# Attention block on one core: group weights in two tiles, a pinned division, v's products in seven of eight key blocks

## The chip, the core and the metric

The kernel runs on one NeuronCore of a Trainium2 chip, in 32-bit floats throughout. The metric is the device time in microseconds of one execution; the profile is one execution under the hardware profiler. Five engines work side by side, each with its own instruction stream: TensorE (PE; its weight loads are shown as PEld), VectorE (DVE), ScalarE (ACT), GpSimd (POOL) and SyncE (SP), which here only issues DMAs. A 32-bit matmul shows as two instructions (two passes) in the trace, so that a product of 128x512 counts twice.

## The reference

Sixteen images `x` of 512 channels and 32 x 32 = 1024 positions go through one attention block. Cut to what is computed:

```python
xn  = (x - mean) * rsqrt(var + 1e-5)          # over each of 8 groups of 64 channels
xn  = xn * gamma + beta
q, k, v = split(qkv_w @ xn + qkv_b)           # each 512 x 1024
# 4 heads of 128 channels
attn = softmax(q.T @ k / sqrt(128))           # 1024 x 1024 for each head
o    = v @ attn.T
out  = x + proj_w @ o + proj_b
```

## The kernel before

**Loop.** The program is one unrolled sequence of steps: image `b` (16), head `h` (4), key block `j` (8 blocks of 128 keys). A step computes `scores` (line 710: 128 keys against 1024 queries in two halves, exponential on ScalarE, running sum of the exponentials `tot` on VectorE at lines 724 and 726) and the `weighted_sum` (line 801) of the step before. After a head's last block, `denominators` (line 728) turns the sum into a 32x32 tile of reciprocals; `spread_inverse` (line 751) writes it to a DRAM row and loads it back to all partitions (`rinv`, DMAs on ScalarE's queue); `divide` (line 815) multiplies the head's output `o` by it, on VectorE. The sums of the projection's operand (`sums_of_b`, line 268, shown as L272 on `o` and `ot`) read the divided outputs.

**Filler.** Between the attention's matmuls stand the projections of other images: q and k of the image's second pair of heads in head 0, the output projection of the image before in head 1, q and k of the next image's first pair in head 2, v of the next image in head 3. `plan_head` (line 947) spreads the units of such a projection over the eight blocks with `spread(plan, units, first, last)` (line 818): unit i goes to block first + i(last - first)/n.

**Projections.** Each is two levels of Strassen's scheme (Winograd's form, seven products in place of eight). The seven outer products go in four groups, `OUTER = ((1, 5), (2, 6), (7, 4), (3,))`: two, two, two and one at a time. A group is `two_levels`' unit list (line 457): seven inner products in the order 1, 2, 6, 5, 7, 4, 3, each followed by its eviction from PSUM (line 421 on ScalarE, line 529 on VectorE) and by outstanding additions (`combine`, line 572). Thus a projection has 28 units; a unit of the last group is half as large. `staggered` (line 842) starts group 1 when group 0 has done four units, group 2 four later, group 3 eight after that, so two groups overlap. Sums of the moving operand are made by VectorE at line 495 (`qk_t`, `pp_t`), or, for v, loaded back from DRAM where q and k of the same image kept them. v's results go through an addition (line 649, `vt`), a 32x32 transpose (line 652, `vu`), a DRAM tile (`vd`) and a load in another order (line 665).

**Weights.** A group's weights are one tile of seven 128x128 blocks for each of its outer products: the four raw blocks a11, a12, a21, a22 and the sums s1, s2, s3, s4, where s3 takes a21's place (`SLOTS`). In image 0 `group_weights` (line 345) makes them from staged raw blocks with VectorE (lines 355 to 375) and stores them in DRAM; later every group loads its tile with one DMA on SyncE's queue (line 350). The pool `w` has two buffers, shared by the groups of all projections:

```python
wpool = ctx.enter_context(tc.tile_pool(name="w", bufs=2))
FACTORS = {1: ("a11", "b11"), 2: ("a12", "b21"), 3: ("s4", "b22"), 4: ("a22", "t4"),
           5: ("s1", "t1"), 6: ("s2", "t2"), 7: ("s3", "t3")}
```

(The first line is line 171; the table is lines 142 to 145.) A tile's buffer comes free when the last product that reads the tile is done, and SyncE's load of a later group waits for that.

**Order.** The framework orders each engine's instructions when the program is built: a planner simulates the engines, takes what it believes to be ready first, and may put an instruction far ahead of its place in the source. On the chip each engine then runs its list in that fixed order and waits at the head of it. `tc.issue_after(ins)` makes the instructions of its block come after `ins` in their engine's list.

Of the kernel before, what the change touches and what calls it, by code (L numbers as in the profile page):

```python
# [10 lines left out]
F32 = mybir.dt.float32  # L11
# [5 lines left out]
P = 128  # L17
# [126 lines left out]
    5: ("s1", "t1"), 6: ("s2", "t2"), 7: ("s3", "t3"),  # L144
}

SLOTS = {"a11": 0, "a12": 1, "a21": 2, "s3": 2, "a22": 3, "s1": 4, "s2": 5, "s4": 6}
KC = 2
Q = 256

# [4 lines left out]
def fast_path(ctx, tc, x, sources, out, consts, flag, dims):  # L155
# [6 lines left out]
    nc = tc.nc  # L162
# [150 lines left out]
    stage, store = {}, {}  # L313
    for site in (*range(PAIRS), "proj", "v"):
        for g, group in enumerate(OUTER):
            store[site, g] = kept.tile(
                [P, len(group), 7, P], F32, name=f"kept_{site}_{g}"
            )

    store["last"] = kept.tile([P, 8, HALF], F32, name="kept_last")  # L320

# [22 lines left out]

    def group_weights(site, g, first):

        group = OUTER[g]
        w = wpool.tile([P, 2, 7, P], F32, tag="w", name=f"w_{site}_{g}")
        if not first:
            nc.sync.dma_start(w[:, : len(group)], store[site, g])  # L350
            return w
        st, raw = stage[site], raw_blocks(site)
        for i, p in enumerate(group):
            n = FACTORS[p][0]
            flat = w[:, i, 0:4, :].rearrange("p s d -> p (s d)")
            if n in raw:
                load_block(w[:, i, 0:4, :], raw[n])
            elif n == "s1":
                nc.vector.tensor_add(flat, st["a21"], st["a22"])
            elif n == "s2":  # L360
                nc.vector.tensor_sub(flat, st["s1"], st["a11"])
            elif n == "s3":
                nc.vector.tensor_sub(flat, st["a11"], st["a21"])
            else:
                nc.vector.tensor_sub(flat, st["a12"], st["s2"])
            if site == "proj":
                nc.sync.dma_start(store["last"][:, p], flat)

        def at(n):
            return w[:, : len(group), SLOTS[n], :]  # L370

        nc.vector.tensor_add(at("s1"), at("a21"), at("a22"))
        nc.vector.tensor_sub(at("s3"), at("a11"), at("a21"))
        nc.vector.tensor_sub(at("s2"), at("s1"), at("a11"))
        nc.vector.tensor_sub(at("s4"), at("a12"), at("s2"))
        nc.sync.dma_start(store[site, g], w[:, : len(group)])
        return w

    wv = {}
# [77 lines left out]
    def two_levels(name, site, b, blocks, finish, sums="make"):  # L457

        R = {}
        haves = [{} for _ in OUTER]

        def part(g, i, row=None):
            t = R[g][:, i]
            return t if row is None else t[:, row, :]

        def group_units(g):
            group = OUTER[g]
            n = len(group)  # L470
            have = haves[g]

            def weights():
                have["w"] = group_weights(site, g, b == 0 and site in range(PAIRS))

            def sum_tile(h, m):
                haves[h][m] = tpool.tile(
                    [P, 2, Q], F32, tag=f"in_{m}", name=f"{name}_{h}_{m}"
                )
                return haves[h][m][:, : len(OUTER[h])]  # L480

            def load(h, m):
                if sums == "load" and h < len(OUTER):
                    nc.sync.dma_start(sum_tile(h, m), inner_kept[b, h, m])

            def inner_sum(m):
                if sums == "load":
                    return
                sum_tile(g, m)
                a, c = {  # L490
                    "t1": ("b12", "b11"), "t2": ("b22", "t1"), "t3": ("t2", "b11"),
                    "t4": ("b21", "t2"),
                }[m]
                for i in range(n):
                    nc.vector.tensor_sub(have[m][:, i, :], inner(i, a), inner(i, c))  # L495
                if sums == "keep":
                    t = dpool.tile([P, n, Q], F32, tag=f"{m}_{g}", bufs=1, name=f"kept_{m}_{g}")
                    inner_kept[b, g, m] = t
                    nc.gpsimd.dma_start(t, have[m][:, :n])  # L499

            def inner(i, m):
                if m[0] == "t":
                    return have[m][:, i, :]
                outer = blocks()[FACTORS[group[i]][1]]
                return outer[int(m[1]) - 1][:, ts(int(m[2]) - 1, Q)]

            def mm(acc, j, first):
                an, bn = FACTORS[j]
                for i in range(n):
                    nc.tensor.matmul(  # L510
                        acc[:, ts(i, Q)], have["w"][:, i, SLOTS[an], :], inner(i, bn),
                        start=(first and i == 0), stop=True, skip_group_check=True,
                    )

            def out_(which, a, c=None):
                row, half = int(which[1]) - 1, int(which[2]) - 1
                if g not in R:
                    R[g] = rpool.tile(
                        [P, 2, 2, HALF], F32, tag=f"r{g % 3}", name=f"{name}_r{g}"
                    )  # L520
                dst = R[g][:, :n, row, ts(half, Q)]

                def view(t):
                    return t[:, : n * Q].rearrange("p (i q) -> p i q", q=Q)

                if c is None:
                    nc.scalar.copy(dst, view(a))
                else:
                    nc.vector.tensor_add(dst, view(a), view(c))  # L529

            p1, p2, p6, p5, p7, p4, p3 = strassen(f"{name}_{g}", mm, out_, n * Q)

            def unit(*steps):
                def one():
                    for f in steps:
                        f()
                    for _ in range(min(len(pending), 2 if g == len(OUTER) - 1 else 1)):
                        pending.pop(0)()
                return one

            def end():
                combine(g)
                if g == len(OUTER) - 1:
                    run(pending)
                    pending.clear()


            return [
                unit(weights, lambda: inner_sum("t1"), lambda: inner_sum("t2"), p1),
                unit(lambda: inner_sum("t3"), p2), unit(lambda: inner_sum("t4"), p6),  # L550
                unit(lambda: load(g + 1, "t2"), p5), unit(lambda: load(g + 1, "t1"), p7),
                unit(lambda: load(g + 1, "t3"), p4),
                unit(lambda: load(g + 1, "t4"), p3, end),
            ]

        def first_loads():
            for m in ("t2", "t1", "t3", "t4"):
                t = tpool.tile([P, 2, Q], F32, tag=f"in_{m}", name=f"{name}_0_{m}")
                haves[0][m] = t
                nc.sync.dma_start(t, inner_kept[b, 0, m])  # L560

        pending = []

        def add(o, i, j):
            pending.append(lambda: nc.vector.tensor_add(part(*o), part(*i), part(*j)))

        def done(which, i, j):
            pending.extend(
                lambda r=r: finish(which, r, part(*i, r), part(*j, r)) for r in range(2)
            )  # L570

        def combine(g):

            if g == 1:
                done("c11", (0, 0), (1, 0))
                add((1, 1), (0, 0), (1, 1))
                add((1, 0), (1, 1), (0, 1))
            elif g == 2:
                add((2, 0), (1, 1), (2, 0))
                done("c22", (2, 0), (0, 1))  # L580
                done("c21", (2, 0), (2, 1))
            elif g == 3:
                done("c12", (1, 0), (3, 0))

        ahead[name] = first_loads
        return [group_units(g) for g in range(len(OUTER))]
# [113 lines left out]


    ps, tot, po, rinv, last_eviction = {}, {}, {}, {}, {}
    inverse, rows_of = {}, {}
    steps = B * HEADS * NB

    def where(s):
# [3 lines left out]
    def scores(s, half):  # L710
# [11 lines left out]
        if j == 1:  # L722
            tot[b, h] = lpool.tile([P, N], F32, tag="tot", name=f"tot_{b}_{h}")
            nc.vector.tensor_add(tot[b, h], ps[s - 1], ps[s])
        else:
            nc.vector.tensor_add(tot[b, h][:, i], tot[b, h][:, i], ps[s][:, i])  # L726

    def denominators(b, h):

# [217 lines left out]
    def plan_head(b, h):  # L947
# [39 lines left out]
        elif h == 2:  # L987
            spread(plan, staggered(qk_groups(b + 1, 0)), 0, NB)
        else:
            spread(plan, staggered(next_v.pop()), 0, NB)  # L990
        return plan

    def warm(n, name):
# [31 lines left out]
    for s in range(steps + 1):  # L1025
# [14 lines left out]
        for half in range(NH2):  # L1040
            if s < steps:
                scores(s, half)
                if j == 1 and s > NB:
                    spread_inverse(*where(s - NB)[:2], half)
                if half == 0 and j == 5 and s > NB:
                    divide(*where(s - NB)[:2])
            if s > 0:
                weighted_sum(s - 1, half)
            n = (len(units) + 1) // 2
# [137 lines left out]
```

## Time and profile before

| what | value |
|---|---|
| median of 8 runs | 3311.57 us (3307.72 to 3318.35) |
| the profiled execution | 3314.3 us, of which the span from first to last instruction is 3312.5 |
| mean granted clock of TensorE | 0.995 |
| TensorE matmul | 3206.3 us busy |
| VectorE | 2659.6 us busy |
| ScalarE | 1446.5 us busy |
| load of a group's weights, 896 KB, for q and k (90 times) | 6.2 us from issue to landing (median) |
| same for v / for the output projection (45 times each) | 4.9 / 4.4 us |
| inverse of the denominators, 512 KB (63 times) | 4.5 us from issue to landing (median), 12.3 at most |
| division of a head's output, 128x1024 (63 times) | 1.22 us |
| v's transposes, 128x512 (120 times) | 1.12 us |

A busy TensorE is not one at its peak, since matmuls are pipelined and their ends are modelled: starts tell more. A wait row such as "A L1 <- B L2: total, times, longest" says how long engine A stood idle before an instruction of line 1 until B's work of line 2 was done. Idle time of an engine costs nothing unless another one waits for it.

### The profile page before, as it was taken

The page shows a single profiled execution, that of the slowest core. Times are in us where ns is not written, and L with a number is a line of the kernel's source. Part 1 is how long each engine was busy: PE and PEld are TensorE (multiplying, and loading weights), DVE is VectorE, ACT ScalarE, POOL GpSimd, SP SyncE. Part 2 cuts the span into 40 slices and gives each one's busy share as a digit, 9 for nine tenths or more (in the row PEclk, how much of TensorE's full clock was granted, in tenths as well). Part 3 has the DMA queues.
Part 4 walks back from the last instruction along what each step waited for, and adds up shares of the span by engine and source line. Part 5 has one row for each costly group of instructions (what it writes and reads, how often), then busy time and mean ns, then how long its engine had stood idle before and what let it go on. Part 6 is the DMA issues. An engine that isn't in the chain of part 4 may idle for free. (4 is left out here: it accounts for less than half of the span.)

```text
span 3312.5 us, 33607 instructions
## 1 busy us (share of the span) xinstructions
PE 3206.3 (97%) x10474; PEld 2169.9 (66%) x10474; DVE 2659.6 (80%) x4609; ACT 1446.5 (44%) x2709; POOL 527.0 (16%) x938
## 2 busy tenths in 40 slices
PE   8999999999999999999999999999999999999999
PEld 6566666666666666666666666666666666666664
DVE  8878878788787887878888787887878878788784
ACT  2534435354353443534435354353534535344342
POOL 1011121111211112111121111212112121121100
PEclk9999999999999999999999999999999999999999
DMA  5555454545535455454554545545355463454631
GB/s 196 199 186 153 168 177 143 167 150 170 170 137 170 145 176 162 158 165 140 173 175 154 169 130 184 162 157 176 133 175 175 145 204 123 162 165 162 185 124 39
DMA packets 172664, 530.54 MB, mean 160 GB/s; under 512 B 28864, under 2 KB 51904, under 8 KB 172480
## 3 DMA queue, kind: packets, MB, share of 16 engines
q1 hardware_dynamic: 91120, 276.86, 25.3%
q0 software_dynamic: 67392, 216.07, 20.1%
q10 hardware_dynamic: 13968, 35.41, 3.4%
q8 instruction: 85, 1.39, 0.2%
q14 instruction: 99, 0.81, 0.1%
HBM read 389.56 MB, written 138.67 MB: 159 GB/s over the span
## 5 line engine op out<-in xcount | busy, mean ns | idle before, releaser
L806 PE MATMUL po<-p,v 128*128 128x512 f32 x2048 | 1056.2, 597 | 0.0
L713 PE MATMUL s<-qk,qk 128*128 128x512 f32 x2048 | 1052.8, 596 | 2.6 <-ACT p L718 2.5
L718 ACT ACTIVATE p<-s 128x512 f32<-128x512 f32 x1024 | 610.1, 596 | 994.3 <-PE s L713 989.3
L806 PEld LDWEIGHTS po<-p,v 128*128 128x128 f32 x2048 | 601.1, 303 | 317.8 <-issue 199.7
L726 DVE TENSOR_TENSOR tot<-tot,p 128x1024 f32<-128x1024 f32 x385 | 469.9, 1221 | 118.9 <-ACT p L718 116.9
L713 PEld LDWEIGHTS s<-qk,qk 128*128 128x128 f32 x2048 | 388.9, 191 | 91.8 <-issue 29.2
L510 PE MATMUL qk_x<-qk_t,w 128*128 128x256 f32 x1344 | 361.7, 386 | 2.3 <-DVE qk_t L495 1.2
L510 PEld LDWEIGHTS qk_x<-qk_t,w 128*128 128x128 f32 x1344 | 247.0, 190 | 175.7 <-issue 66.4
L421 ACT COPY qk_u<-qk_x 128x512 f32<-128x512 f32 (+1 forms) x256 | 136.3, 533 | 288.1 <-PE qk_x L510 246.1
L499 POOL DMA_DIRECT2D kept_t<-qk_t x256 | 138.8, 543 | 495.5 <-DVE qk_t L495 461.5
L660 POOL DMA_DIRECT2D vd<-vu x120 | 66.5, 554 | 827.6 <-DVE vu L652 767.4
L529 DVE TENSOR_TENSOR qk_r<-qk_y,qk_u 128x512 f32<-128x512 f32 (+1 forms) x256 | 158.5, 619 | 45.6 <-ACT qk_u L421 24.6
L510 PE MATMUL pp_x<-pp_t,w_proj 128*128 128x256 f32 x630 | 173.8, 389 | 2.8 <-ACT pp_u L421 2.8
L529 DVE TENSOR_TENSOR v_r<-v_y,v_u 128x512 f32<-128x512 f32 (+1 forms) x120 | 74.9, 624 | 124.9 <-ACT v_u L421 117.3
L510 PE MATMUL qk_y<-qk_t,w 128*128 128x256 f32 x448 | 130.7, 398 | 43.4 <-DVE qk_t L495 29.7
L697 POOL DMA_DIRECT2D out_y<-y x120 | 66.4, 554 | 653.4 <-DVE y L696 620.6
L510 PEld LDWEIGHTS v_x<-v_t,w_v 128*128 128x128 f32 x630 | 118.4, 190 | 79.1 <-issue 38.3
L510 PE MATMUL v_x<-v_t,w_v 128*128 128x256 f32 x630 | 166.6, 381 | 0.0
L510 PEld LDWEIGHTS pp_x<-pp_t,w_proj 128*128 128x128 f32 x630 | 113.8, 190 | 69.5 <-ACT pp_u L421 24.6
L665 POOL DMA_DIRECT2D v<-vd x240 | 140.3, 592 | 52.2 <-issue 46.8
L510 PEld LDWEIGHTS qk_y<-qk_t,w 128*128 128x128 f32 x448 | 81.9, 193 | 99.2 <-DVE qk_t L495 41.3
L510 PE MATMUL qk_y<-x,w 128*128 128x256 f32 x512 | 143.4, 382 | 1.5 <-DVE qk_r L529 1.5
(204 smaller groups left out, 4468.8 us busy)
## 6 DMA issues: line engine op xcount, KB each, us to landing
w<-kept SPq DMA_DIRECT2D x90, 896.0 KB, 6.2
kept_t<-qk_t POOLq DMA_DIRECT2D x192, 256.0 KB, 2.9
v_t<-kept_t SPq DMA_DIRECT2D x180, 256.0 KB, 2.7
w_v<-kept_v SPq DMA_DIRECT2D x45, 896.0 KB, 4.9
w_proj<-kept_proj SPq DMA_DIRECT2D x45, 896.0 KB, 4.4
rinv<-row ACTq DMA_DIRECT2D x63, 512.0 KB, 4.5
x<-in_x POOLq DMA_DIRECT2D x60, 512.0 KB, 5.6
vd<-vu POOLq DMA_DIRECT2D x120, 256.0 KB, 2.6
```

Source lines behind the costliest of these rows:

```text
L421: nc.scalar.copy(t[n][:, :width], t["x"][:, :width])
L499: nc.gpsimd.dma_start(t, have[m][:, :n])
L510: nc.tensor.matmul(acc[:, ts(i, Q)], have["w"][:, i, SLOTS[an], :], inner(i, bn), start=(first and i == 0), stop=True, skip_group_check=True,)
L529: nc.vector.tensor_add(dst, view(a), view(c))
L660: nc.gpsimd.dma_start(rows[which][ts(h, P), :], u)
L665: nc.gpsimd.dma_start(vs[b, pair][ts(q, BLK), half].rearrange("m h (k i) j -> m (h k) (i j)", k=n), rows[which].rearrange("(k m) (q e) -> ...
L697: nc.gpsimd.dma_start(out[b, ts(o, P), ts(half, HALF)], t)
L713: nc.tensor.matmul(sc, ks[b, h][:, ts(j, P)], qs[b, h][:, ts(half, HALF)], start=True, stop=True)
L718: nc.scalar.activation(ps[s][:, ts(half, HALF)], sc, AF.Exp, scale=SCALE)
L726: nc.vector.tensor_add(tot[b, h][:, i], tot[b, h][:, i], ps[s][:, i])
L806: nc.tensor.matmul(po[b, h][:, i], v_block(b, h, j), ps[s][:, i], start=(j == 0), stop=(j == NB - 1),)
```

## The change

There are three parts.

1. A group's weights become two tiles with two buffers each: one of four blocks (a11, a12, s1, s2), read by the products 1, 2, 6 and 5, and one of three (a21 or s3, a22, s4), read by 7, 4 and 3. Loads, stores and, in image 0, the making of raw rows go by tile.
2. The division moves in the source from block 5, first half, to block 4, second half, and stands behind that block's addition to `tot` (`added`) in VectorE's list.
3. The units of v's projection are spread over blocks 0 to 6 of head 3 in place of 0 to 7.

```diff
-SLOTS = {"a11": 0, "a12": 1, "a21": 2, "s3": 2, "a22": 3, "s1": 4, "s2": 5, "s4": 6}
+SLOTS = {
+    "a11": (0, 0), "a12": (0, 1), "s1": (0, 2), "s2": (0, 3),
+    "a21": (1, 0), "s3": (1, 0), "a22": (1, 1), "s4": (1, 2),
+}
+PARTS = (4, 3)
...
         for g, group in enumerate(OUTER):
-            store[site, g] = kept.tile(
-                [P, len(group), 7, P], F32, name=f"kept_{site}_{g}"
-            )
+            for t, m in enumerate(PARTS):
+                store[site, g, t] = kept.tile(
+                    [P, len(group), m, P], F32, name=f"kept_{site}_{g}_{t}"
+                )
...
-        w = wpool.tile([P, 2, 7, P], F32, tag="w", name=f"w_{site}_{g}")
+        n = len(group)
+        w = [
+            wpool.tile([P, 2, m, P], F32, tag=f"w{t}", name=f"w{t}_{site}_{g}")
+            for t, m in enumerate(PARTS)
+        ]
         if not first:
-            nc.sync.dma_start(w[:, : len(group)], store[site, g])
+            for t in range(2):
+                nc.sync.dma_start(w[t][:, :n], store[site, g, t])
             return w
...
-            flat = w[:, i, 0:4, :].rearrange("p s d -> p (s d)")
-            if n in raw:
-                load_block(w[:, i, 0:4, :], raw[n])
-            elif n == "s1":
-                nc.vector.tensor_add(flat, st["a21"], st["a22"])
+            for t in range(2):
+                rows = w[t][:, i, 0:2, :]
+                flat = rows.rearrange("p s d -> p (s d)")
+                if name in raw:
+                    nc.sync.dma_start(
+                        rows, raw[name][:, ts(t, P)].rearrange("(k p) d -> p k d", p=P)
+                    )
+                    continue
+
+                def of(m):
+                    return st[m][:, ts(t, 2 * P)]
+
+                if name == "s1":
+                    nc.vector.tensor_add(flat, of("a21"), of("a22"))
...
-        nc.sync.dma_start(store[site, g], w[:, : len(group)])
+        for t in range(2):
+            nc.sync.dma_start(store[site, g, t], w[t][:, :n])
         return w
...
                 an, bn = FACTORS[j]
+                t, slot = SLOTS[an]
                 for i in range(n):
                     nc.tensor.matmul(
-                        acc[:, ts(i, Q)], have["w"][:, i, SLOTS[an], :], inner(i, bn),
+                        acc[:, ts(i, Q)], have["w"][t][:, i, slot, :], inner(i, bn),
...
-            nc.vector.tensor_add(tot[b, h][:, i], tot[b, h][:, i], ps[s][:, i])
+            added[b, h, j] = nc.vector.tensor_add(
+                tot[b, h][:, i], tot[b, h][:, i], ps[s][:, i]
+            )
...
-            spread(plan, staggered(next_v.pop()), 0, NB)
+
+            spread(plan, staggered(next_v.pop()), 0, NB - 1)
...
-                if half == 0 and j == 5 and s > NB:
-                    divide(*where(s - NB)[:2])
+                if half == 1 and j == 4 and s > NB:
+
+                    with tc.issue_after(added[b, h, 4].ins):
+                        divide(*where(s - NB)[:2])
```

More of the change, by code (lines that the diff above doesn't have):

```diff
@@ L353, in group_weights, with at @@
         for i, p in enumerate(group):
-            n = FACTORS[p][0]
-            flat = w[:, i, 0:4, :].rearrange("p s d -> p (s d)")
-            if n in raw:
-                load_block(w[:, i, 0:4, :], raw[n])
-            elif n == "s1":
-                nc.vector.tensor_add(flat, st["a21"], st["a22"])
[L360 to L365, printed above, removed]
-            if site == "proj":
-                nc.sync.dma_start(store["last"][:, p], flat)
-        def at(n):
-            return w[:, : len(group), SLOTS[n], :]
+            name = FACTORS[p][0]
+            for t in range(2):
[10 more added lines that the diff above has]
+                    nc.vector.tensor_add(flat, of("a21"), of("a22"))
+                elif name == "s2":
+                    nc.vector.tensor_sub(flat, of("s1"), of("a11"))
+                elif name == "s3":
+                    nc.vector.tensor_sub(flat, of("a11"), of("a21"))
+                else:
+                    nc.vector.tensor_sub(flat, of("a12"), of("s2"))
+            if site == "proj":
+                for t in range(2):
+                    nc.sync.dma_start(
+                        store["last"][:, p, ts(t, 2 * P)],
+                        w[t][:, i, 0:2, :].rearrange("p s d -> p (s d)"),
+                    )
+        def at(m):
+            t, slot = SLOTS[m]
+            return w[t][:, :n, slot, :]
         nc.vector.tensor_add(at("s1"), at("a21"), at("a22"))
@@ L375, in group_weights @@
         nc.vector.tensor_sub(at("s4"), at("a12"), at("s2"))
-        nc.sync.dma_start(store[site, g], w[:, : len(group)])
+        for t in range(2):
+            nc.sync.dma_start(store[site, g, t], w[t][:, :n])
         return w
@@ L702, in fast_path @@
     ps, tot, po, rinv, last_eviction = {}, {}, {}, {}, {}
-    inverse, rows_of = {}, {}
+    inverse, rows_of, added = {}, {}, {}
     steps = B * HEADS * NB
@@ L725, in scores @@
         else:
-            nc.vector.tensor_add(tot[b, h][:, i], tot[b, h][:, i], ps[s][:, i])
+            added[b, h, j] = nc.vector.tensor_add(
+                tot[b, h][:, i], tot[b, h][:, i], ps[s][:, i]
+            )
     def denominators(b, h):
```

## The prediction

> **What bounds the kernel now.** I read the page's first part, the waits of TensorE, the answers for the weights' tile and for the division's line, then windows and timelines of one image. From the page, the span and the busy shares:
>
> ```profile
> span 3312.5 us, 33607 instructions
> PE 3206.3 (97%) x10474; PEld 2169.9 (66%) x10474; DVE 2659.6 (80%) x4609; ACT 1446.5 (44%) x2709; POOL 527.0 (16%) x938
> ```
>
> TensorE is busy for 97% of the span, so only what makes it stand still, or run at half clock, can be won. The waits view of TensorE (us in total, times, longest) lists what makes it stand still:
>
> ```profile
> PE qk_y L510 <- DVE qk_t L495: 29.7, 27, 3.0
> PE qk_x L510 <- DMA w<-kept: 23.2, 18, 2.0
> PE qk_y L510 <- DVE qk_r L529: 15.5, 14, 4.5
> ...
> PE v_y L510 <- DVE v_r L529: 5.4, 15, 0.4
> ```
>
> Four rows, 73.8 us together. Row 2 is late weights; the others are late work of VectorE. Row 4 comes 15 times, once an image. The division's own row, in the answer for its line, is VectorE standing in its own queue:
>
> ```profile
>   DMA rinv<-row: 82.8, 33
> ```
>
> Next, image 3's head 0, cut into its key blocks 0, 1, 2, 3 and 4 to 7 (columns: length, then busy time of PE, PEld, DVE, ACT, POOL, clock, DMA share, GB/s), and below it head 3 of image 2, blocks 0 to 4 and 5 to 7:
>
> ```profile
> 661.40:667.00 5.60, 5.60 (x20) 3.90 (x19) 5.60 (x8) 2.63 (x5) 1.97 (x4) 1.00 0.94 271
> 667.00:676.20 9.20, 7.74 (x28) 4.99 (x27) 8.83 (x26) 3.27 (x6) 5.46 (x10) 1.00 0.63 197
> 676.20:683.80 7.60, 7.18 (x26) 4.97 (x25) 4.57 (x8) 2.37 (x4) 3.57 (x7) 1.00 1.04 285
> 683.80:689.80 6.00, 6.00 (x22) 4.25 (x21) 5.39 (x11) 2.37 (x4) 0.00 (x0) 1.00 0.63 244
> 689.80:712.70 22.90, 22.90 (x75) 15.62 (x74) 20.01 (x33) 8.39 (x16) 0.54 (x1) 1.00 0.25 83
> ```
> ```profile
> 612.00:644.70 32.70, 32.70 (x113) 23.65 (x112) 19.19 (x30) 13.01 (x22) 0.00 (x0) 1.00 0.50 158
> 644.70:661.40 16.70, 16.33 (x52) 10.62 (x51) 16.10 (x21) 6.14 (x12) 6.05 (x11) 1.00 0.63 191
> ```
>
> VectorE is 59% busy through the first five blocks of v's head (19.19 of 32.70), then full for three blocks and two more of the next head. TensorE idles in block 1 (9.20 - 7.74 = 1.46 us) and block 2 (0.42). The timeline around these two shows which instructions:
>
> ```profile
> 667.99 1.09 DVE L652 STREAM_TRANSPOSE vu<-vt 128x512 f32<-128x512 f32 x1
> ...
> 669.45 0.70 PE L510 MATMUL qk_y<-qk_t,w 128*128 128x256 f32 x2 [1.46 <-DVE qk_t L495]
> ...
> 680.18 1.23 DVE L816 TENSOR_TENSOR o<-o,rinv 128x1024 f32<-128x1024 f32 x1 [3.00 <-DMA rinv<-row]
> 681.44 0.69 DVE L272 TENSOR_TENSOR ot<-o,o 128x512 f32<-128x512 f32 x1
> 682.05 0.68 DVE L529 TENSOR_TENSOR qk_r<-qk_y,qk_p 128x512 f32<-128x512 f32 x1
> 682.66 0.68 DVE L529 TENSOR_TENSOR qk_r<-qk_y,qk_u 128x512 f32<-128x512 f32 x1
> 683.25 0.68 DVE L272 TENSOR_TENSOR ot<-ot,o 128x512 f32<-128x512 f32 x1
> ```
>
> The planner has hoisted the division (written at block 5) to block 2, where the inverse has not landed; the queue behind it waits 3.00 us, and with it the addition that frees the bank qk_y. And v's last transposes stand before the sums qk_t that a product of the next image needs.
>
> [...] in the windows 788 to 792, 1301 to 1305, 1816 to 1820 and 3137 to 3145, each beginning at one of the stalls above, the clock is 0.69, 0.57, 0.62 and 0.57. [...]
>
> **Part one, weights in two tiles.** A group's four first products (1, 2, 6, 5) read a11, a12, s2, s1: the first tile. The last three read the second. Only two groups' weights fit, so group 2 loads into group 0's place. Now SyncE may issue it after group 0's seventh product: at 578.74 in image 2's head 2, it lands 6.7 us later, and group 2 starts at 585.58 after 1.69 us of waiting. With the split the first tile is free after group 0's fourth product. Three more products of each of groups 0 and 1 (0.86 us each by their starts in the timeline: 579.42, 580.28, 581.15) and about a block of attention (four matmuls, each 0.86 by the same starts, so 3.44) lie between: an estimate of 6 x 0.86 + 3.44 = 8.6 us earlier, against 1.69 late. The second tile loads at the old time but is needed four products later, 4 x 0.86 + 3.44 = 6.9 us or more. Gain: nearly the whole row, 0.9 x 23.2 = 21 us (upper end 31.5, with the 8.3 us that weight loads waited for it). Costs: the bytes are the same, in packets of 4096 and 3072 instead of 7168 (19.96 B/ns for 4096 against 21.55); 240 more issues of 0.32 us on SyncE, which does nothing else and mostly waits. One more wait at each group's fifth product: between nothing and 0.06 us x 240 = 14 us, by an extra wait instruction of 51 ns; I take nothing, since single waits cost no start-to-start time in this trace. In the first image 16 additions of 128x512 (0.68 us) become 32 of 128x256 (0.42): 16 x 0.16 = 2.6 us of VectorE, hidden but for about 1 us. [...]
>
> **Part two, the pinned division.** It now stands behind block 4's addition. Its inverse was issued at 672.55 and landed at 680.2, so at block 4 (from 689.8) the wait is gone: row 3, 15.5 us. Behind it come three sums L272 (3 x 0.69), so 1.22 + 2.07 = 3.3 us move into blocks 4 to 7, where VectorE has 22.90 - 20.01 = 2.9 us free and, in blocks 2 and 3, 3.0 + 3.3 us are freed. TensorE needs these sums in head 1, from 712.7: they should be done by about 703. If this cover were gone, additions behind them would be late by up to 3.3 us. I take 0.75 x 15.5 = 12 us. In head 1 the division (1.22 us) now stands before the next image's statistics, which gate its normalisation: between 15 x 1.22 = 18 us lost and, as it leaves block 2 free for proj's additions, the 1.9 us that TensorE waits for those (pp_y) won; I take 5 lost. Heads 2 and 3 have VectorE time to spare there.
>
> **Part three, v in seven blocks.** 28 units go 4, 4, 4, 4, 4, 4, 4, 0 instead of 4, 3, 4, 3, 4, 3, 4, 3. The products end about 3 half units and half an attention block earlier: 3 x 0.43 + 1.7 = 3 us, and VectorE gets work into the blocks where it was 59% busy. Block 7 then holds only attention, 3.44 us, for which VectorE owes one addition (1.22). Row 4: 0.8 x 5.4 = 4 us. The 1.46 us at the seam: 15 x 1.46 = 22 us of row 1; an advance of 2 to 3 us covers it if VectorE's backlog moves as far. I take 0.6 x 22 = 13 us. The rest of row 1 lies in head 2 and stays.
>
> **Clock.** The four half-clock windows lose 4 x 0.31 + 4 x 0.43 + 4 x 0.38 + 8 x 0.43 = 7.9 us; I take 5.
>
> **Sum.** 21 + 12 + 4 + 13 + 5 - 5 - 1 = 49. The profiled span is 3312.5 us (3314.3 with what lies around it); 3263.5 after. The runs' median, 3311.57, lies 0.9 below the span: **3263 us**, its own range 3250 to 3282.
>
> **Rivals.** (A) VectorE takes over: the weights' wait goes, but the seam and the bank stay late because the planner lays the queue anew. For: in head 0 VectorE is 44.41 busy of 51.3. Against: 6.9 us are free there. Gain 21 + 4 + 2 = 27, less 3: 3288. (B) Everything goes: 23.2 + 15.5 + 22 + 5.4 + 7.9 = 74, plus the upper end for the weights, 8: 3230. (C) Nothing changes, the gains hidden because another wait follows each at once: 3305 to 3318. Against: after 585.58 VectorE stood 2.42 us idle, so it was not next. (D) Slower: in head 0 the division and its sums hold up each addition behind them by 3.3 us, and in head 1 by 1.22, 4.5 us an image, 68 in all; against 21 + 4 + 13 + 5 = 43 this gives 3337. It decides from 43/15 = 2.9 us an image. The 2.9 us free in blocks 4 to 7 speak against it.
>
> **How the numbers follow.** Forecast 0.50, A 0.22, B 0.08, C 0.07, D 0.13. The range 3233 to 3306 holds the forecast, A and most of B and leaves out D, most of C and the tail of B. About 0.2% (6.6 us) is what a measurement can tell from no change: faster 0.80, same 0.06, slower 0.14.
>
> **What would show it.** The row w<-kept gone from TensorE's waits; loads of 512 and 384 KB; the division in block 4 without a wait for rinv; VectorE fuller in v's first five blocks; block 1 of head 0 near 7.7 us; a clock above 0.995. Wrong it would be by new rows of qk_r or pp_r on TensorE in blocks 5 to 7 of head 0 or in head 1, or by later normalised x at head 2.

## The result, and the profile after

The changed kernel takes 3296.02 us (median of 11 runs) against 3311.64 us (32 runs of the kernel before): a ratio of 0.9954, 95% interval 0.9944 to 0.9964. It is faster, by 15.6 us, a third of the forecast gain of 49, and lies in the upper part of the predicted range, nearest to rival A's 3288.

The page's first part, of the kernel after:

```profile
span 3296.7 us, 34096 instructions
PE 3203.3 (97%) x10474; PEld 2178.5 (66%) x10474; DVE 2640.7 (80%) x4625; ACT 1445.3 (44%) x2709; POOL 527.1 (16%) x938
```

TensorE stood still for 3296.7 - 3203.3 = 93.4 us where it had been 3312.5 - 3206.3 = 106.2; that is 12.8 of the 15.8 us by which the span fell. The mean clock is 0.994 (before 0.995). The waits view of TensorE (us in total, times, longest), kernel after:

```profile
PE qk_x L538 <- DVE qk_t L522: 36.7, 30, 2.3
PE qk_y L538 <- DVE qk_r L557: 11.4, 15, 2.1
...
PE v_y L538 <- DVE v_r L557: 9.1, 15, 0.6
PE pp_x L538 <- ACT pp_p L448: 6.5, 14, 1.5
...
PE qk_y L538 <- DVE qk_t L522: 3.4, 10, 0.4
```

The row of late weights, 23.2 us before, is gone: parts one and two did to their own rows what they say. But three other rows have grown: waits for the moving sums `qk_t` from 29.7 + 1.2 to 36.7 + 3.4, for v's bank from 5.4 to 9.1, for proj's products from 2.8 (`pp_u`) to 6.5 (`pp_p`). The row of `qk_r` fell only from 15.5 to 11.4, and it is another wait: before, 13.5 us of it lay in block 2 of head 0; now 11.0 lie in block 2 of head 2.

The windows of image 3's head 0, blocks 0, 1, 2 and 4 to 7, and below them blocks 0 to 4 of head 3 before it, kernel after (columns as for the kernel before):

```profile
657.70:667.30 9.60, 7.39 (x26) 4.86 (x25) 9.52 (x18) 2.95 (x5) 5.17 (x10) 1.00 0.55 174
667.30:675.00 7.70, 7.70 (x22) 4.61 (x21) 4.61 (x14) 2.86 (x5) 3.76 (x7) 0.78 0.99 235
675.00:681.90 6.90, 6.90 (x26) 5.05 (x25) 4.51 (x6) 2.37 (x4) 2.17 (x4) 1.00 0.77 249
...
687.90:710.80 22.90, 22.90 (x75) 15.64 (x74) 20.92 (x32) 8.40 (x16) 0.54 (x1) 1.00 0.29 94
```
```profile
608.00:641.50 33.50, 33.50 (x117) 24.36 (x116) 18.83 (x29) 13.02 (x22) 0.74 (x2) 1.00 0.51 155
```

Block 1 takes 7.70 us without a gap, as I expected for it, but the gap has only moved into block 0: 9.60 us long, 2.21 of it idle, where before it took 5.60 and had none. Blocks 0 and 1 together take 17.3 us where they took 14.8. The 0.78 in block 1 is half clock behind that gap: 0.5 for 3.4 us, from 667.47 on. In the first five blocks of v's head VectorE is 18.83 of 33.50 busy, 56%, where it was 59%. This hides two opposite moves. By tile, averaged over images 1 to 14, the pin took the division and its three sums, 3.3 us, out of these blocks into blocks 5 to 7, and 2.9 us of v's additions and transposes came in.

The timeline of the kernel after around that gap:

```profile
662.29 1.22 DVE L763 STREAM_TRANSPOSE tt<-tot 128x1024 f32<-128x1024 f32 x1
663.43 1.04 DVE L680 STREAM_TRANSPOSE vu<-vt 128x512 f32<-128x512 f32 x1
664.32 1.16 DVE L765 TENSOR_REDUCE part<-tt 128x32 f32<-128x1024 f32 x1
...
665.40 0.41 DVE L522 TENSOR_TENSOR qk_t<-x,qk_t 128x256 f32<-128x256 f32 x1
...
665.96 1.48 PE L538 MATMUL qk_x<-qk_t,w 128*128 128x256 f32 x4 [2.10 <-DVE qk_t L522]
```

The planner has taken the next image's products forward into block 0; the sum they read stands on VectorE behind the first two instructions of the old head's denominators (`tt`, `part`) and v's last transpose, 3.4 us of work. And the division, in its pinned place:

```profile
693.60 1.22 DVE L754 TENSOR_TENSOR tot<-tot,p 128x1024 f32<-128x1024 f32 x1
694.74 1.22 DVE L846 TENSOR_TENSOR o<-o,rinv 128x1024 f32<-128x1024 f32 x1
```

It follows the addition of block 4 at once and waits for nothing.

Below, the seam is the border of two images, head 3 to head 0. Sums by place ("the seam costs ...") are TensorE's idle time before the instructions there, added up from the trace over images 1 to 15; a row runs over the whole program. The seam costs 22.0 us in the kernel before and 33.2 in the kernel after. A head's excess is its length less the usual start-to-start distances of TensorE's instructions in it. Over the 15 images it was 59.1, 19.2, 52.2 and 17.5 us in heads 0 to 3, and is 57.9, 15.9, 38.3 and 22.4. So nearly all that the change won, it won in head 2, and head 0, at which two of its three parts aim, gained 1.2 us.

### The profile page after: what moved, and what is told of

The parts are those of the page before. It is cut to its first block, busy times and chain, and to the rows that moved or that the text cites. A ratio compares the mean times of both kernels' runs of the same rounds, so it can differ in the third digit from the quotient of the medians.

```text
span 3296.7 us, 34096 instructions
## 1 busy us (share of the span) xinstructions
PE 3203.3 (97%) x10474; PEld 2178.5 (66%) x10474; DVE 2640.7 (80%) x4625; ACT 1445.3 (44%) x2709; POOL 527.1 (16%) x938
## 4 chain that ended last, share of the span: by engine, by line
PE 38%; issue 38%; DVE 11%; DMA 7%; POOL 6%; ACT 0%; POOLq 0%; SPq 0%; ACTq 0%; DVEq 0%
PE po L836 10%; PE s L741 10%; PE qk_x L538 5%; POOL kept_t L526 4%; DMA vd<-vu 4%; PE qk_y L538 4%; PE pp_x L538 4%; PE pp_y L538 3%; DMA out_y<-y 2%; DVE xt L277 2%; DMA y<-in_x 1%; DVE tot L754 1%; DVE vu L680 1%; DVE part L765 1%; DVE tt L763 1%
## 5 line engine op out<-in xcount | busy, mean ns | idle before, releaser
L538 PE MATMUL qk_x<-qk_t,w 128*128 128x256 f32 x1344 | 363.3, 387 | 41.1 <-DVE qk_t L522 36.7
L693 POOL DMA_DIRECT2D v<-vd x240 | 140.3, 592 | 76.9 <-issue 67.5
L448 ACT COPY v_u<-v_x 128x512 f32<-128x512 f32 (+1 forms) x124 | 66.3, 535 | 165.2 <-PE v_x L538 126.4
L625 DVE SCALAR_TENSOR_TENSOR qk<-qk_r,qkb_sb,qk_r 128x512 f32<-128x512 f32 x192 | 137.1, 741 | 1.1
```

The source lines that it names most:

```text
L448: nc.scalar.copy(t[n][:, :width], t["x"][:, :width])
L538: nc.tensor.matmul(acc[:, ts(i, Q)], have["w"][t][:, i, slot, :], inner(i, bn), start=(first and i == 0), stop=True, skip_group_check=True,)
L625: nc.vector.scalar_tensor_tensor(st[b, h][:, ts(half, HALF)], a, qkb_sb[:, i : i + 1], c, ALU.add, ALU.add)
L693: nc.gpsimd.dma_start(vs[b, pair][ts(q, BLK), half].rearrange("m h (k i) j -> m (h k) (i j)", k=n), rows[which].rearrange("(k m) (q e) -> ...
```

## The experiments

Theory one: the pinned division of head 2, with its three sums, stands where VectorE is full in head 3, and eats what the seven blocks give. Theory two: the planner moves the next image's products forward by as much as v ends earlier, so that their sums are late whatever the division does. A third reading, that the denominators stand in VectorE's list ahead of the sums, came later and has its own runs. The first five runs do one part alone or leave one out.

Each ratio is against the kernel before in the same session. Its median moved from 3311.64 to 3317.75 us between sessions, so runs of different sessions are compared by their ratios, and ratios whose intervals overlap are not told apart. Sums by place come from one execution of each kernel.

**Two tiles alone** (the changed kernel, division and v's spread as before).

```diff
-                if half == 1 and j == 4 and s > NB:
-                    with tc.issue_after(added[b, h, 4].ins):
-                        divide(*where(s - NB)[:2])
+                if half == 0 and j == 5 and s > NB:
+                    divide(*where(s - NB)[:2])
...
-            spread(plan, staggered(next_v.pop()), 0, NB - 1)
+            spread(plan, staggered(next_v.pop()), 0, NB)
```

> The weights in two tiles alone, division and v as before. Both theories: TensorE's wait for w<-kept (23.2 us before) falls below 3 us. If that gain stays, the time is 3311.6 - 21 = 3290 us or so, 3285 to 3297. If another wait takes it over in head 2 (sums of x or the bank qk_y), 3300 to 3310.

Measured: 3333.48 against 3316.01 us, ratio 1.0052 (1.0038 to 1.0067): slower, which neither theory had, though the row of late weights fell from 23.2 to 1.9 us. TensorE's waits, and the division's own wait in the answer for its tile `rinv`, two tiles alone:

```profile
PE qk_y L538 <- DVE qk_t L522: 37.7, 29, 4.0
PE qk_y L538 <- DVE qk_r L557: 35.6, 16, 4.4
```
```profile
  DMA rinv<-row: 124.7, 35
```

The bank `qk_y` behind the waiting division costs 35.6 us where it cost 15.5, and the division waits 124.7 us where it waited 82.8. The timeline of image 3, head 0, shows why:

```profile
674.96 0.32 SPq L362 DMA_DIRECT2D w<-kept  x1
...
675.79 0.33 ACTq L790 DMA_DIRECT2D rinv<-row  x1
...
685.83 1.23 DVE L846 TENSOR_TENSOR o<-o,rinv 128x1024 f32<-128x1024 f32 x1 [4.81 <-DMA rinv<-row]
```

The first tile's load, which can now start earlier, is issued 0.8 us ahead of the inverse's. From the inverse's issue to the division it takes 10.0 us; in the kernel before it took 7.6 (672.55 to 680.18), with no load of weights just ahead. The other images agree: in head 0 the inverse lands 10.0 us after its issue (median of 15), with a load of weights issued 0.1 to 1.6 us ahead every time, where it took 8.1 before. That the two loads contend fits the order and the times; no run moved one of them alone, so it is not shown.

**The pin alone** (the kernel before, division as in the change).

```diff
...
-                if half == 0 and j == 5 and s > NB:
-                    divide(*where(s - NB)[:2])
+                if half == 1 and j == 4 and s > NB:
+                    with tc.issue_after(added[b, h, 4].ins):
+                        divide(*where(s - NB)[:2])
```

> The pinned division alone. It takes VectorE's wait for rinv (82.8 us before) to about 0 and the wait of qk_y for qk_r in block 2 of head 0 (15.5 us) with it. If that is all, the time is 0.5% below the kernel before, 3293 to 3302 where that one is at 3312. If late weights fill the place (they stay in one tile here), w<-kept rises from 23 us to over 30 and the time is 3304 to 3314.

Measured: 3324.78 against 3317.75 us, 1.0025 (1.0014 to 1.0036): slower, and outside both expectations. The division's wait is gone, but this row of TensorE's waits has taken more than its place (before: 29.7, 27 times):

```profile
PE qk_y L510 <- DVE qk_t L495: 51.9, 15, 3.6
```

Fifteen times, once a seam, and 3.6 us at most. In head 3 the pin sets the division and the three sums behind it, 1.23 + 0.70 + 0.68 + 0.68 = 3.3 us by the timeline, into the blocks where VectorE was full already, and everything behind them is late at the seam by about 2 us (51.9 us over the 15 seams; before 22.0). Half clock follows: 78.5 us of it against 27.3, without the window in which the program ends; mean clock 0.988.

**Seven blocks alone** (the kernel before).

```diff
-            spread(plan, staggered(next_v.pop()), 0, NB)
+            spread(plan, staggered(next_v.pop()), 0, NB - 1)
```

> v's products in seven blocks alone. Theory one (the pinned division of head 2, with its three sums of o, stands in VectorE's full stretch of head 3 and eats what the seven blocks give): without the pin the wait of a q/k product at the seam of two images falls from 1.5 us an image below 0.8, time 3292 to 3302. Theory two (the planner moves the next image's products forward by as much as v ends earlier, so their sums are late whatever the division does): the seam's wait is 1.5 to 2.6 us in the first blocks of head 0, time 3306 to 3320.

Measured: 3307.51 against 3316.01 us, 0.9970 (0.9958 to 0.9983). The profiled execution lies 0.3% below the median, so its rows say where and not how much:

```profile
PE qk_x L510 <- DVE qk_t L495: 33.5, 30, 2.0
```

The seam costs 32.3 us, more than the 22.0 before: the step fails alone as it does in the whole, as theory two has it. But VectorE did get v's work earlier. Head 3 before image 3, blocks 0 to 4:

```profile
612.30:645.80 33.50, 33.50 (x117) 24.37 (x116) 21.48 (x33) 12.84 (x22) 0.78 (x2) 1.00 0.53 171
```

VectorE is busy for 64% here where it was 59%. Counted from head 0's first score product (medians of 15 seams), v's last transpose ends after 5.7 us instead of 7.7. But 16 instead of 10 of the q and k instructions now stand in block 0, the first of them that stalls is reached after 5.3 us instead of 6.6, and the denominators' first transpose starts at 5.6 instead of 1.7, just in front of the sum for it. What is won is elsewhere. In head 0's block 2 the wait for the bank falls from 13.5 to 1.3 us, with the division's own wait in that head (48.5 to 9.2), and v's bank costs 1.6 instead of 5.0.

**The change with v's products in eight blocks.**

```diff
-            spread(plan, staggered(next_v.pop()), 0, NB - 1)
+            spread(plan, staggered(next_v.pop()), 0, NB)
```

> The changed kernel with v in eight blocks again. Theory one: the seam gets worse, since the division still stands in the full stretch and nothing is given back: 3300 to 3312. Theory two: seven blocks were what spoiled the seam, so 3270 to 3288.

Measured: 3296.43 us, 0.9938 (0.9925 to 0.9951) against the same 3316.01. The whole change has 0.9954, with an overlapping interval: leaving part three out changes nothing that can be told. This is in neither theory's range. The seam costs 34.2 us.

**The change with head 3's division at its old place.**

```diff
-                if half == 1 and j == 4 and s > NB:
+                if h == 3:
+                    if half == 0 and j == 5:
+                        divide(*where(s - NB)[:2])
+                elif half == 1 and j == 4 and s > NB:
```

> The changed kernel, but in head 3 the division stands where it stood before (block 5 in the source, no pin). Theory one: 3.2 us leave VectorE's full stretch, the seam's wait falls from 2.4 us an image below 1, and half-clock windows go with it: 3262 to 3280. Theory two: the seam stays as it is, 3292 to 3300.

Measured: 3296.12 us, 0.9937 (0.9924 to 0.9950). No difference, so theory one missed: what the pin costs in head 3 in the kernel before, taking it away does not bring back in the changed kernel. The seam costs 37.8 us.

**The pin in heads 0 to 2 alone** (the kernel before, with the edit just shown in place of the plain pin).

> The kernel before with the division pinned in heads 0, 1 and 2 but not in head 3. If the pin alone is slower because in head 3 it puts the division and three sums of o, 3.3 us, into VectorE's full stretch, the seam's wait falls from 3.6 us an image back to about 1.6 and the clock from 0.988 to 0.995: 3295 to 3308 where the kernel before is at 3316. If the pin spoils the seam from head 0, the wait stays above 3 us an image and the time at 3318 to 3328.

Measured: 3294.48 against 3316.04 us, 0.9927 (0.9912 to 0.9942). This one edit brings at least what the whole change brings, and 1.0% more than the pin in all heads. Out of head 3, the pin leaves the seam as it was, at 22.0 us. A row of its waits of TensorE:

```profile
PE qk_x L510 <- DMA w<-kept: 38.4, 26, 3.7
```

With the division out of the way, TensorE stands at the next late thing, a group's weights: 38.4 us where it was 23.2. In head 0 the bank's 13.5 us in block 2 are gone, and the weights in block 3 cost 18.8 where they cost 4.9; that head's excess is 59.8 us, no less than before. The gain lies in head 2 (15.0 us less excess) and in head 1 (4.5).

**Two tiles and the pin in heads 0 to 2, v in eight blocks** (both edits on the changed kernel).

> Weights in two tiles and the division pinned in heads 0 to 2, v in eight blocks. If seven blocks are what made the seam worse (43 us of waiting there with this very pin), it stays at 25 us here and the late weights (38 us with the pin alone) go: 3258 to 3276 where the kernel before is at 3316. If the two tiles make the seam worse by their earlier loads, as they made the division's wait worse, its wait is over 35 us again and the time 3285 to 3298.

Measured: 3289.93 against 3316.27 us, 0.9923 (0.9910 to 0.9936). The time lies in the range of the reading that the tiles spoil the seam, but the seam's wait lies where the other had it. Against the pin alone (0.9927) the two tiles add nothing that can be told, although they take away a row of 38.4 us. Two rows of its waits of TensorE:

```profile
PE qk_y L538 <- DVE qk_t L522: 33.1, 28, 4.1
PE qk_y L538 <- DVE qk_r L557: 13.6, 15, 2.2
```

Of the first, 25.7 us lie at the seam. The rest and nearly all of the second lie in head 2's block 2, where waits for sums and the bank, 23.5 us in all, stand in place of the late weights (19.5 us with the pin alone). Head 0 wins 18.3 us of excess by the two tiles, head 2 loses 10.5, and head 3 loses 3.7.

Four kernels with the two tiles can now be set side by side: head 3 pinned or not, v in seven blocks or eight. The seam costs 33.2 us with the pin and seven blocks (the change), 34.2 with the pin and eight, 37.8 with seven blocks and no pin, and 25.7 with neither. So either one is enough to make the seam late, and this is why taking away one alone, as two runs above did, mended nothing. In time the last kernel is hardly better (0.9923 against 0.9938 and 0.9937), since its head 2 has some 8 us more excess than theirs; why that is so isn't shown.

**Denominators behind the next image's first sums** (the changed kernel; head 0 only).

```diff
-        if 0 < s < steps and s % NB == 0:
+        behind = s < steps and j == 0 and b > 0 and h == 0
+        if 0 < s < steps and s % NB == 0 and not behind:
             denominators(*where(s - 1)[:2])
...
             run(units[half * n : (half + 1) * n])
+            if half == 0 and behind:
+                with tc.issue_after(newest["t2"].ins):
+                    denominators(*where(s - 1)[:2])
```

(`newest` keeps the instructions that make t1 and t2, the first two differences of the moving operand.)

> The changed kernel, with the denominators of head 3 put behind the first sums (t1, t2) of the next q and k in VectorE's list. If the seam's wait comes from VectorE's order (3.3 us of transpose, sum and reciprocal stand ahead of these sums), it falls from 2.4 us an image below 0.5 and most half-clock windows at the seam go: 3250 to 3275. If VectorE's backlog of v's transposes is the cause, whatever the order, the wait only moves to another product in blocks 0 to 1: 3288 to 3300.

Measured: 3265.49 against 3317.75 us, 0.9841 (0.9824 to 0.9857), 1.1% better than the change, as the reading from the order had it. The row that had grown to 36.7 us is

```profile
PE qk_x L540 <- DVE qk_t L522: 11.8, 31, 1.2
```

At the seam, 8.3 us are left of 33.2.

The same with v in eight blocks:

> The same with v in eight blocks. If seven blocks bring anything once the order is mended, this is slower than the one with seven by 10 us or more; if not, within 6 us of it.

Measured: 3277.41 us, 0.9879 (0.9860 to 0.9899), with 26.9 us in that row. Here seven blocks are worth 12 us; that v's own last transposes are next in the way, and end earlier with seven, is the likely reason, but it wasn't shown apart, and the last pair of runs below has no such difference.

**V's 120 transposes left out** (the changed kernel; what is stored of v is not transposed, so the output is another one).

```diff
-            nc.vector.transpose(
-                u.rearrange("p (q i j) -> p j q i", q=n, i=BLK),
-                t.rearrange("p (j q i) -> p j q i", q=n, i=BLK),
-            )
+            u = t
```

> The changed kernel with v's 120 transposes left out: v is stored untransposed, so the attention's output is another one. It takes 120 x 1.1 = 132 us of work from VectorE, nearly all of it in its full stretch around the seam. If that stretch causes the seam's wait, it falls from 37 us to below 8 and the time to 3240 to 3262; if not, it stays above 20 us.

Measured, in a single execution: 3228.67 us, the row of `qk_x` at 3.5 us where it was 36.7. This is 67 us for 120 x 1.12 = 134 us of VectorE, so about half of what VectorE was spared came back as time. Head 0 is left with 2.1 us of excess. So VectorE's queue before the seam is the cause of that wait; the order in the queue, which the run before mends, decides how much of it is felt.

**The order alone** (the kernel before, with the denominators behind the sums in head 0 and the division unpinned).

> The kernel before with nothing but the denominators of head 3 behind the next q and k's first sums. If the order at the seam is a cause of its own, its wait (24 us) falls below 8 us and the time by 15 to 30 us, to 3286 to 3302. But the inverse comes some 2 us later here and the division still stands in block 2, so its wait may rise by as much: then 3300 to 3316.

Measured: 3351.64 against 3316.04 us, 1.0116 (1.0101 to 1.0130). Slower than either reading had it. The seam is mended (the whole row of `qk_t` is 8.7 us), but the inverse is now issued 15.3 us after head 0's first score product, not 10.6 (medians of 15), and the unpinned division waits for it at block 2, 80.2 us in that head where it waited 48.5:

```profile
PE qk_y L512 <- DVE qk_r L531: 54.2, 17, 7.4
```

So the order needs a division that stands later, which here is the pin; the order with the pin and without the two tiles was not run.

**The order, with head 3 unpinned:**

> The mended order (denominators behind the first sums) on the changed kernel, with the division of head 3 left unpinned. If the division in VectorE's full stretch still costs, 3245 to 3260; if it costs nothing once the order is mended, within 4 us of 3265.

Measured: 3271.95 us, 0.9865 (0.9851 to 0.9880): not better than with the pin in head 3 (0.9841). So that pin does no harm here, where the seam is mended.

**The order in heads 0 and 2**, which both begin q and k products (condition `h in (0, 2) and b + 1 < B`).

> The same order in head 2 as well as in head 0. If the waits in block 2 of head 2 (22 us in all) come from the denominators ahead of the sums there too, 3245 to 3257; if they come from stores of the kept sums and the bank, 3262 to 3272.

Measured: 3253.57 against 3316.04 us, 0.9813 (0.9800 to 0.9826), the fastest kernel here: 62 us off the kernel before. Its timeline at image 3's seam, and its waits of TensorE:

```profile
658.51 0.72 DVE L522 TENSOR_TENSOR qk_t<-qk_t,x 128x256 f32<-128x256 f32 x2
...
659.77 1.22 DVE L765 STREAM_TRANSPOSE tt<-tot 128x1024 f32<-128x1024 f32 x1
```
```profile
PE qk_y L540 <- DVE qk_t L522: 12.5, 14, 1.0
PE qk_x L540 <- DVE qk_t L522: 12.1, 18, 2.3
```

The sums stand ahead of `tt`, and the row of `qk_r` that had moved into head 2 is down to one wait of 0.5 us; what is left in head 2 are the 12.5 us for `qk_t`, now in block 1. The mean clock is 0.999. With v in eight blocks and head 3 unpinned it is as fast:

> The same with the denominators behind the first sums in heads 0 and 2. If mending the order is worth as much without the seven blocks, 3240 to 3256, that is at or below the best so far (0.981 of the kernel before); if the seven blocks are needed for it, 3256 to 3270.

Measured: 3253.81 against 3316.27 us, 0.9818 (0.9803 to 0.9832).

The edits don't add up: alone they give +0.52%, +0.25% and -0.30%, together -0.46%. The two tiles and the pin mend each other's side effect: with the tiles alone the inverse lands later (10.0 us after its issue in head 0 instead of 8.1), but the pinned division does not need it early (it waits 0.0 us in all pinned heads), and the weights, later still with the pin in heads 0 to 2, are what the tiles cure.

## Why the prediction was wrong in size

Three steps failed, each a slack that the prediction counted on and that was not there: that nothing stands behind the late weights, that VectorE has time to spare in head 3, and that the seam is covered when VectorE's backlog ends earlier. The third has the wrong sign.

**Part one, the weights: mechanism right, gain nearly nil.** The loads do go earlier and the row goes. Two things were missed. The prediction priced packets and issues, but not what is issued right behind the earlier load: the inverse, which took 10.0 us instead of 7.6 with such a load just ahead (two tiles alone, image 3). In the whole change no load of weights is issued in the last 4 us ahead of head 0's inverse; it took 6.4 us there (median of 15), and the pinned division did not wait. And its keeping "0.9 x 23.2 = 21 us" rests on one place, after 585.58, where VectorE "was not next". In head 2 it was: late weights cost 18.1 us there, and after the change the waits in head 2's block 2 for `qk_r` and `qk_t` cost 11.0 + 3.4 + 2.3 = 16.7. The denominators are a cause here too: moving them behind the sums in head 2 took those waits away, and left 12.5 us in block 1 (0.9841 to 0.9813). Over the pin in heads 0 to 2, the two tiles measured 0.0004 of the time, 1 us with overlapping intervals, in place of 21.

**Part two, the pin: its own row right, its place wrong.** The division waits no more, as forecast. In heads 0 to 2 alone the pin gave 0.73%, 24 us, where the sum had 12 - 5 = 7, but that it gave more is luck: in head 0, where the 12 were to come from, late weights took all of it, and the gain came in heads 1 and 2. "Heads 2 and 3 have VectorE time to spare there" was the step that failed: the prediction's own windows had VectorE 16.10 of 16.70 us busy in head 3's blocks 5 to 7. Pinned in all heads instead of three it cost 1.0%, about 32 us (1.0025 against 0.9927). In the changed kernel this loss isn't seen, since the seven blocks make the seam as late by themselves. The feared loss in head 1 did not come: its median length went from 50.3 to 49.6 us, against 5 us in all charged to it. Some 0.4 of these 0.7 us are two product instructions that now start in head 2; by excess head 1 won 3.3 us in all.

**Part three, seven blocks: the step with the wrong sign.** "An advance of 2 to 3 us covers it if VectorE's backlog moves as far." Alone, the backlog did move: VectorE got its work in the blocks where it was 59% busy (64%), and v's last transposes ended 2.0 us earlier. But products that end earlier let the planner put the next image's products earlier, not only v's sums: they arrived 1.3 us earlier and found the denominators just ahead of their sums. The seam rose from 22.0 to 32.3 us, and in the whole change to 33.2: -11.2 in place of +13. V's bank, +4 in the sum, was right alone (5.0 to 1.6). In the whole it rose to 8.4, and moved from block 7 to block 5, where the division and its sums now stand; with head 3 unpinned it is 1.7. In the change as a whole the part is worth nothing (eight blocks: the same time), because the pin in head 3 is enough to make the seam late.

**Clock.** Taken at +5; half-clock time rose from 27.3 to 37.5 us, which by the half clock is about 5 lost. The four windows of the prediction hold 17.1 of the 27.3 us: it left out 6.8 us from 980.7 on, and 3.4 in image 0. The stalls at its windows were 1.9 to 4.5 us long, and the half clock at them lasted 3.4 us three times and 6.8 once.

**The rivals.** A named what happened ("the seam and the bank stay late because the planner lays the queue anew") and was 8 us off. That it came so near is partly luck, since it kept 21 us for the weights, which did not stay. The argument against it, that VectorE has 6.9 us free in head 0, looks at the wrong place, since the seam waits for a queue that is full for a few microseconds, whatever is free later. D feared for blocks 4 to 7 of head 0; they held: VectorE is 20.92 of 22.90 us busy there and nothing waits. C's mechanism, another wait behind each, is what the weights met in head 2.

What stays open: of the 62 us that the fastest kernel gains, TensorE's idle time accounts for 106.2 - 67.5 = 38.7 us and its busy time for 25.1 (3206.3 to 3181.2). Half clock, 27.3 to 6.8 us, explains some 10 of the latter. The rest was not taken apart, nor was the gain of the two tiles tried with the order mended and nothing else. Whether, and why, a weights load just ahead makes the inverse land later is open too.

## What to carry to other kernels

When a wait is removed, look in each stage at what stands next in the queue of the engine that feeds it, and count a saving only where that one has slack there and then; a share averaged over a head says nothing on a queue that is full for three blocks. If work is made to end earlier, ask what else the planner will then start earlier, and what that will wait for. Where leaving out one edit changes nothing, leave out the other suspect too: two edits can each be enough for the same loss. Where a load can start earlier, find what else is in flight at its new time, and whether something waits for that. Where work of a finished stage (here the denominators) precedes the first operands of the next in one engine's list, turning that order round may be worth more than all local edits, provided that the finished stage's own reader is put late enough.

## What the hardware showed

- A load of 512 KB (the inverse) with a 512 KB load of weights issued at most 1.6 us ahead, on another queue, took 10.0 us to land (median of 15 in head 0, two tiles alone) instead of 8.1 in the kernel before, with no such load ahead. The division's wait grew from 82.8 to 124.7 us with it, and the row of the bank behind it from 15.5 to 35.6. That the one load delayed the other was not shown.
- Stalls of TensorE of 1.5 us and more often went over into half clock, shorter ones almost never. In the 16 traces, after the first 240 us and without the last 20, there are 97 stretches of half clock, 78 of 3.4 us and 19 of 6.8, and a stall of TensorE stands at the beginning of each. Of the stalls of 0.3 to 1.5 us 1 of 801 led to one, of 1.5 to 2.0 us 16 of 67, of 2.0 to 2.5 us 39 of 66, of 2.5 us and more 41 of 50. The granted clock in such a stretch is 0.5 (0.78 over the 7.70 us of block 1 above, which hold one), and two passes of 128x512 take 1.71 us from start to start in it (668.77 to 670.48, kernel after) where they take 0.86 at full clock (695.64 to 696.50); so, by estimate, a stretch of 3.4 us loses 1.7 us beside the stall. In the pin alone, with fifteen stalls of up to 3.6 us, there are 78.5 us of half clock; in the fastest kernel 6.8.
- The time of single edits on this program is not additive, in sign either: two edits that each make it slower alone (+0.52% and +0.25%) are part of a change that makes it faster (-0.46%).
